# Block 0's x in four slots, its LayerNorm by two, its turns between the rows of shift and scale, and gate's row ahead of a root

## The chip, the core and the metric

The kernel runs on one core of one Trainium2 chip. The metric is the device time of one execution in microseconds. Of the kernel before, three executions took 575.44, 575.63 and 576.18 us; the median is 575.63.

## What is computed

One block of a conditioned network on x of 2 x 2048 x 512 in float32, with a condition of 2 x 512. Six vectors per batch entry come from the condition: shift, scale and gate for each of two halves.

```python
emb = jnp.dot(silu(t), ada_w) + ada_b
shift_msa, scale_msa, gate_msa, shift_mlp, scale_mlp, gate_mlp = jnp.split(emb, 6, axis=-1)
norm = _ln(x) * (1.0 + scale_msa[:, None]) + shift_msa[:, None]
h = gelu(jnp.dot(norm, ssm_w1) + ssm_b1, approximate=False)
x = x + gate_msa[:, None] * (jnp.dot(h, ssm_w2) + ssm_b2)
norm2 = _ln(x) * (1.0 + scale_mlp[:, None]) + shift_mlp[:, None]
hf = gelu(jnp.dot(norm2, ff_w1) + ff_b1, approximate=True)
x = x + gate_mlp[:, None] * (jnp.dot(hf, ff_w2) + ff_b2)
```

`_ln` takes the mean away and multiplies by the reciprocal root of the variance plus 1e-6. `ada_w` is 512 x 3072, the ssm weights are 512 x 512, the ff weights 512 x 1024 and 1024 x 512.

## The kernel before

The 4096 tokens are eight blocks of 512. A block stands as 128 partitions with C = 4 slots of one token each (128 x 4 x 512, 1 MB). Per block there are four products: hA (first ssm weight) and oA (second), then hC and oC for the ff half. Each is computed with seven products of quarters instead of eight (P1 to P7), with sums and differences of quarters formed by DVE and GpSimd ahead of them (nS, hSA, w_s, forms). The hardware order of every engine is the order in which the program is written; the table PLAN says at which product ("P1" and so on) which side work of the first blocks is issued.

What matters here is the beginning, block 0 up to the first product of block 1.

- **Loads.** SP issues them in the order of the program. load_x(0, 2) loads block 0's x in two halves of two slots (line 305). load_ada_01 (348) and load_last_ada_01 (355) load the rows of ada_w for shift and scale of the ssm half, cut by k, a quarter of the 512 rows: k 0 and 1 together, k 2, and k 3 in two halves of columns. Between them come the halves of w1 (323), then x of block 1 (305), gate's columns ada_2 (311), four small rows of gate's bias (376), w2 (318) and so on. ACT issues four small loads of rows into fw2_t: the condition, ada_b, ssm_b1, ff_b1 (336 to 339).
- **Completion counters.** Every transfer counts up one of eight counters (DMAHW0 to DMAHW7), taken in turn over both queues; the issue that takes a counter again stands until the transfer that had it before has landed, and with it everything behind it on SP's queue.
- **Condition.** TensorE turns the 44 rows (1660), ACT copies them to colsT and takes SiLU (1666, 1669). idle matmuls (warm, 1651) keep TensorE busy while it waits. rows_01 (418) multiplies the condition by ada's rows of one k into the bank pada_01; modulation_01 (431, 435) turns the result on DVE and adds the bias, half by half (part 0 wants k 3's first half, part 1 its second).
- **LayerNorm of block 0.** DVE takes statistics per slot (748, 749), n1[0].root() forms variance plus eps (812) and GpSimd raises it to -0.5 (813); first_steps refines the root with four small DVE operations on all four slots (836 to 840). normal writes the normalized slot, on ACT for slots 0 and 2 (876), on DVE for 1 and 3 (880), into blocks. TensorE turns each slot with four matmuls against the identity into the banks pt (911), and modulate scales and shifts from there into nT (932 on ACT, 934 on DVE). h 0 holds slots 0 and 1, h 1 slots 2 and 3.
- **Gate and block 1.** gate_2.0 multiplies the condition by ada_2 on TensorE (397) and adds the bias on DVE (455, result w2_t); gate_2.1 spreads it over the partitions with TensorE (462, pgate), and DVE folds it into w2 (550). n1_1.stats, root, rest, normal, turn, move and modulated are the LayerNorm of block 1: sums and squares on ACT (777, 788), one slot on DVE (748), the root (812, 813), refining steps (853 to 861), normalization (876), turning by DVE in blocks of 32 x 32 (887) and sixteen DMAs (895) instead of TensorE, and modulation (932, 934).

Of the kernel before, what the change touches and what calls it, by code (L numbers as in the profile page):

```python
# [36 lines left out]
F32 = mybir.dt.float32  # L37
AF = mybir.ActivationFunctionType
ALU = mybir.AluOpType
EPS = 1e-06  # L40
# [100 lines left out]
        "P1": "n1_1.stats.0 n1_1.stats.2 n1_0.sum.1 n1_1.stats.1 n1_0.sum.3 n1_1.stats.3",  # L141
        "P2": "n1_0.sum.2 n1_1.stats.4",
        "P5": "n1_1.stats.7 n1_1.stats.6",
        "P6": "n1_1.stats.5 n1_1.root.0 gate_2.0 n1_1.rest.0 n1_1.normal.0",
        "P7": "gate_2.1 n1_1.normal.3 gb_2.0 seed_0.0 gb_2.1 w2.0",
        "P3": "w2.1 seed_0.1 n1_1.turn.0 w2.2 w2.3 w2.4",
        "P4": "n1_1.normal.1 w2.5 n1_1.normal.2",
# [95 lines left out]
def kernel(  # L243
# [57 lines left out]
    def load_x(i, pieces=1):  # L301
        xs[i] = big_tile(f"x_{i}")
        for s in range(pieces):
            c = slice(s * C // pieces, (s + 1) * C // pieces)
            nc.sync.dma_start(out=xs[i][:, c, :], in_=x_blk[i][:, c, :])
# [29 lines left out]
    rows = brows[:ROWS, 2, :P]  # L335
# [76 lines left out]
    def rows_01(pa, ks, hs=range(2)):  # L412

        for k in ks:
            w = ada_01[k // 2][:, k % 2].rearrange("p (g h n m q) -> p h m g n q", g=2, h=2, n=KD // 2, q=G)
            for h in hs:
                for m in range(P // G):
                    nc.tensor.matmul(
                        pa[m * G : (m + 1) * G, h * P : (h + 1) * P],
                        silu[:, k, :],  # L420
                        w[:, h, m],
                        start=(k == 0 and h == 0),
                        stop=(k == KD - 1),
                        tile_position=(0, m * G),
                        skip_group_check=True,
                    )
# [308 lines left out]
    class Norm:  # L735
# [91 lines left out]
            v.tensor_tensor(self.nmr, self.mv[:, :, 0], self.rstd, ALU.mult)  # L827
            v.tensor_scalar(self.nmr, self.nmr, -1.0, None, ALU.mult)

        def first_steps(self):  # L830

            n, v = self.name, nc.vector
            self.rstd, self.nmr = [small.tile([P, C], F32, tag=t, name=f"{t}{n}") for t in ("rstd", "nmr")]
            room = ps_t.tile([P, D], F32, tag="t", name=f"small{n}")
            a, b = room[:, :C], room[:, C : 2 * C]
            v.tensor_scalar(a, self.mv[:, :, 1], EPS, None, ALU.add)
            v.tensor_tensor(b, self.r, a, ALU.mult)
            v.scalar_tensor_tensor(b, b, -0.5, self.r, ALU.mult, ALU.mult)
            v.scalar_tensor_tensor(self.rstd, b, 1.5, self.r, ALU.add, ALU.mult)
            v.scalar_tensor_tensor(self.nmr, self.mv[:, :, 0], -1.0, self.rstd, ALU.mult, ALU.mult)  # L840
# [793 lines left out]
    n1 = {0: Norm(0, 1), 1: Norm(1, 1)}  # L1634
# [14 lines left out]
    def warm(count, blocks=2):  # L1649
        for _ in range(count):  # L1650
            nc.tensor.matmul(
                idle[:, :blocks],
                ident,
                ident.unsqueeze(1).to_broadcast([P, blocks, P]),
                start=True,
                stop=True,
            )

    warm(IDLE - 1, C)
    nc.tensor.transpose(pt[:, :ROWS], rows, ident[:ROWS, :ROWS])  # L1660
# [549 lines left out]
```

## Time and profile before

The profile shows one execution; its own time is 576.39 us, and its span, from the first to the last instruction, is 574.3 us. Names in it lack buffer numbers: x is any block's x, nT any turned block, fw_t is fw2_t, w_t is w2_t.

| | us |
|---|---|
| executions | 575.44, 575.63, 576.18 |
| the profiled execution | 576.39 |
| its span | 574.3 |
| DVE busy | 443.5 |
| ACT busy | 306.2 |
| GpSimd busy | 452.8 |
| DMA: moved, mean rate | 61.79 MB, 108 GB/s |

In the timeline a row has start and length in us, the engine, the line, the operation, output and inputs, and in brackets how long the engine stood idle before it and what it waited for. SPq and ACTq are the queues' issues of DMAs, PEld TensorE's loads of weights. The first 32 us move 11.52 MB, 360 GB/s in the mean; after that the DMA engines are mostly idle.

### The profile page before, as it was taken

How to read it: one execution, taken by the hardware profiler on the slowest of the kernel's cores; microseconds unless marked ns; L12 is line 12 of the kernel's file. 1: busy time of each engine (PE TensorE's matmuls, PEld its weight loads, DVE VectorE, ACT ScalarE, POOL GpSimd, SP SyncE). 2: the span in 40 equal slices, each digit the busy share in tenths (PEclk: the TensorE clock that was granted, in tenths of full speed). 3: DMA queues.
4: the chain of work that ended last, by engine and by line, in shares of the span. 5: the costliest groups of instructions: out<-in, count | busy, mean ns of one | idle time of the engine just before them, and what ended most of it. 6: DMA issues, size and time to landing. Idle time of an engine off the chain costs nothing.

```text
span 574.3 us, 10316 instructions
## 1 busy us (share of the span) xinstructions
PE 568.2 (99%) x3495; PEld 512.4 (89%) x3495; DVE 443.5 (77%) x992; ACT 306.2 (53%) x612; POOL 452.8 (79%) x477
## 2 busy tenths in 40 slices
PE   8999999999999999999999999999999999999997
PEld 4888888898899889998899988998889999899897
DVE  4898899657789376986869877996768588897676
ACT  2628559566834875448724688335655431732430
POOL 1699897996897869897899989998993888379261
PEclk9999999999999999999999999999999999999999
DMA  8968330414305503383032921242240240031002
GB/s 318 392 199 285 93 87 6 98 54 179 68 9 155 212 2 74 102 260 117 1 92 63 349 86 24 51 126 114 92 110 1 111 136 14 0 74 75 0 1 74
DMA packets 26992, 61.79 MB, mean 108 GB/s; under 512 B 5136, under 2 KB 6716, under 8 KB 25276
## 3 DMA queue, kind: packets, MB, share of 16 engines
q1 hardware_dynamic: 23040, 55.67, 30.0%
q10 hardware_dynamic: 3900, 5.47, 3.8%
q8 instruction: 28, 0.46, 0.3%
q14 instruction: 24, 0.20, 0.1%
HBM read 35.42 MB, written 9.97 MB: 79 GB/s over the span
## 4 chain that ended last, share of the span: by engine, by line
PE 97%; DMA 2%; DVE 0%; SPq 0%; ACT 0%; issue 0%; DVEq 0%
PE px_hC L1530 12%; PE pv_hC L1530 10%; PE py_hC L1530 10%; PE py_hA L709 9%; PE pl_oC_A_y L1364 5%; PE pv_hA L709 5%; PE py_oA L1091 5%; PE pl_oC_P_y L1204 4%; PE pl_oC_B_y L1364 4%; PE py_oA L709 4%; PE py_oC L1156 4%; PE pl_oC_A_v L1364 2%; PE px_hA L709 2%; PE pl_oC_P_v L1204 2%; PE pl_oA_y L1106 2%; PE pl_oC_B_v L1364 2%
## 5 line engine op out<-in xcount | busy, mean ns | idle before, releaser
L1435 POOL TENSOR_TENSOR forms<-forms 128x256 f32<-128x256 f32 x64 | 47.0, 735 | 3.8
L813 POOL TENSOR_TENSOR r<-ve,minus_half 128x4 f32<-128x4 f32 x16 | 16.6, 1037 | 41.4 <-DVE ve L812 33.8
L1530 PE MATMUL py_hC<-forms,fw 128*128 128x256 f32 x192 | 46.7, 380 | 0.0
L932 ACT ACTIVATE nT<-nT,mod,mod 128x512 f32<-128x512 f32 x31 | 22.9, 804 | 42.3 <-DMA nT<-blocks 34.3
L1530 PEld LDWEIGHTS py_hC<-forms,fw 128*128 128x128 f32 x192 | 36.3, 190 | 5.2 <-DVE hClo L1547 0.2
L1547 DVE TENSOR_TENSOR hClo<-hClo,py_hC 128x512 f32<-128x512 f32 x46 | 31.1, 682 | 10.6 <-ACT hClo L1544 7.4
L500 POOL TENSOR_TENSOR hSC<-hClo,hChi 128x512 f32<-128x512 f32 x14 | 18.0, 1286 | 27.0 <-ACT hChi L1525 24.8
L876 ACT ACTIVATE nT<-x,nmr,rstd 128x512 f32<-128x512 f32 x33 | 24.9, 804 | 18.8 <-DVE nmr L861 16.6
L1547 DVE TENSOR_TENSOR hChi<-hChi,pv_hC 128x512 f32<-128x512 f32 x38 | 25.2, 677 | 9.6 <-PE pv_hC L1530 5.3
L748 DVE BATCH_NORM_STATS2 st<-x 128x6 f32<-128x512 f32 x41 | 27.7, 677 | 5.6 <-DMA x<-in_x_dram 5.5
L1530 PE MATMUL px_hC<-forms,fw 128*128 128x256 f32 x128 | 31.5, 379 | 0.0
L1525 ACT ACTIVATE hClo<-hClo,colsT 128x256 f32<-128x256 f32 x64 | 28.8, 498 | 5.0 <-DVE hClo L1547 4.8
L1525 ACT ACTIVATE hChi<-hChi,colsT 128x256 f32<-128x256 f32 x64 | 28.7, 496 | 2.9 <-DVE hChi L1547 2.9
L1530 PEld LDWEIGHTS px_hC<-forms,fw 128*128 128x128 f32 x128 | 24.3, 190 | 3.3
L500 POOL TENSOR_TENSOR hClo<-hClo 128x512 f32<-128x512 f32 (+1 forms) x21 | 26.1, 1241 | 0.1
L1547 DVE TENSOR_TENSOR hChi<-hChi,px_hC 128x512 f32<-128x512 f32 x32 | 21.8, 682 | 4.4 <-ACT hClo L1544 2.1
L932 ACT ACTIVATE x<-x,mod 128x512 f32<-128x512 f32 x24 | 17.6, 802 | 13.4 <-DMA x<-blocks 13.4
L887 DVE STREAM_TRANSPOSE blocks<-nT 128x512 f32<-128x512 f32 x36 | 24.0, 691 | 0.7 <-ACT nT L876 0.7
L1530 PE MATMUL px_hC<-forms,fw_s 128*128 128x256 f32 x96 | 23.6, 382 | 0.0
L1544 ACT ACTIVATE hClo<-px_hC 128x512 f32<-128x512 f32 x22 | 13.1, 596 | 19.5 <-PE px_hC L1530 16.0
L1547 DVE TENSOR_TENSOR hClo<-hClo,px_hC 128x512 f32<-128x512 f32 x26 | 17.6, 677 | 7.6 <-PE px_hC L1530 7.0
L1530 PE MATMUL pv_hC<-nT,fw 128*128 128x256 f32 x96 | 23.3, 379 | 0.0
(588 smaller groups left out, 1904.5 us busy)
## 6 DMA issues: line engine op xcount, KB each, us to landing
x<-in_x_dram SPq DMA_DIRECT2D x13, 1024.0 KB
out_dram<-x SPq DMA_DIRECT2D x14, 512.0 KB
x<-blocks SPq DMA_DIRECT2D x93, 64.0 KB
nT<-blocks SPq DMA_DIRECT2D x88, 64.0 KB
ada<-in_L_cond_ada_w_dram SPq DMA_DIRECT2D x5, 1024.0 KB
fw<-in_L_cond_ff_w_dram SPq DMA_DIRECT2D x2, 2048.0 KB
nT<-blocks ACTq DMA_DIRECT2D x56, 64.0 KB
w<-in_L_cond_ssm_w_dram SPq DMA_DIRECT2D x2, 1024.0 KB
```

The lines of the kernel that those rows point to most:

```text
L500: eng.tensor_tensor(out[:, r], a[:, r], b[:, r], f)
L709: nc.tensor.matmul(ps[b][j * apart][:, j, :], lhs(p, j, k), rhs(p, j, k), start=(fresh and j * (not apart) == 0 and k == 0), stop=(p in (" ...
L748: nc.vector.bn_stats(st, xs[self.i][:, c, :])
L876: nc.scalar.activation(t, x_c, AF.Identity, bias=self.nmr[:, c : c + 1], scale=self.rstd[:, c : c + 1])
L932: nc.scalar.activation(dst, src, AF.Identity, bias=shift, scale=scale)
L1091: nc.tensor.matmul(ps[BANK[p]][:, j, :], hops(p, j, k), wops[p][:, k, :], start=False, stop=(k == KD // 2 - 1), skip_group_check=True,)
L1204: nc.tensor.matmul(t[:, n, :], hops.leaves[p][f][:, k, :], leaf_wops[p][f][:, k, :], start=room not in started, stop=(f in ("P2", "P3", "P ...
L1364: nc.tensor.matmul(rooms[g, b][:, at[p], :], hops.leaves[p][f][:, k, :], leaf_wops[p][f][:, k, :], start=(g, b) not in started, stop=(f in ...
L1435: eng.tensor_tensor(reg[d], reg[a], reg[b], ALU.add if f == "+" else ALU.subtract)
L1525: nc.scalar.activation(h, h, AF.Gelu_apprx_tanh, bias=fb1T[:, m : m + 1])
L1530: nc.tensor.matmul(ps[b][:, j, :], fa[ra][:, j * P : (j + 1) * P], fb[rb].rearrange("p a (c q) -> p c a q", q=Q), start=(fresh and j == 0) ...
L1547: nc.vector.tensor_tensor(dest(d), dest(d), ps[b], op)
```

## The change

Five edits. Block 0's x is loaded in four transfers of one slot. The rows of k 0, 1 and 2 become one transfer each. The condition's eight rows are turned by themselves, ahead of the 44, with one idle matmul of 512 columns and one of 128 columns fewer in all, and SiLU reads them from the bank. The root and its refining steps run once for slots 0 and 1 and once for slots 2 and 3, the additions of 1 to colsT go from DVE to GpSimd between the two roots, and on TensorE the turns of slots 1 and 0 go ahead of the rows of k 2, with only slots 3 and 2 behind the first half of k 3. In PLAN, gate_2.0 goes ahead of block 1's root.

```diff
-        "P6": "n1_1.stats.5 n1_1.root.0 gate_2.0 n1_1.rest.0 n1_1.normal.0",
+        "P6": "n1_1.stats.5 gate_2.0 n1_1.root.0 n1_1.rest.0 n1_1.normal.0",
...
-    load_x(0, 2)
+    load_x(0, C)
...
-    load_ada_01((0, 1))
-    load_ada_01((2,))
+    for k in range(KD - 1):
+        load_ada_01((k,))
...
+        def first_root(self, h):
+
+            n, v, s = self.name, nc.vector, slice(h * C // 2, (h + 1) * C // 2)
...
+            v.tensor_scalar(self.ve[:, s], self.mv[:, s, 1], EPS, None, ALU.add)
+            nc.gpsimd.tensor_tensor(self.r[:, s], self.ve[:, s], minus_half[:, s], ALU.pow)
+            v.tensor_scalar(self.first_room[:, s], self.mv[:, s, 1], EPS, None, ALU.add)
...
-    warm(IDLE - 1, C)
+    warm(IDLE - 3, C)
+    turned_cond = pt[:, ROWS : ROWS + B * KD]
+    nc.tensor.transpose(turned_cond, rows[R_COND:R_ADA], ident[: B * KD, : B * KD])
+    warm(1, C)
     nc.tensor.transpose(pt[:, :ROWS], rows, ident[:ROWS, :ROWS])
     warm(1, C)
-    warm(1, 1)
-
-    run(n1[0].stats())
-    n1[0].root()
-    nc.scalar.copy(colsT, pt[:, :ROWS])
...
+    nc.scalar.copy(colsT[:, R_ADA:], pt[:, R_ADA:ROWS])
+
+    stats = n1[0].stats()
+    run(stats[:2])
+    n1[0].first_root(0)
+    run(stats[2:])
+    for g in (1, 4):
+        rows_g = colsT[:, R_ADA + g * KD : R_ADA + (g + 1) * KD]
+        nc.gpsimd.tensor_scalar(rows_g, rows_g, 1.0, None, ALU.add)
+    n1[0].first_root(1)
     w1_ops, w1_sums, w1_s = weight_of_first("w1", w1_sb)
     run(w1_sums)
+    for h in range(2):
+        n1[0].first_steps(h)
+        for c in (3 * h, 1 + h):
+            n1[0].normal(c, nc.vector if c % 2 else None, on_pe=True)
     pada_01 = ps_t.tile([P, D], F32, tag="t", name="pada_01")
-    rows_01(pada_01, (0, 1))
-    for c in range(C):
-        n1[0].normal(c, nc.vector if c % 2 else None, on_pe=True)
...
+    rows_01(pada_01, (0, 1))
+    n1[0].transpose(1, pts, True)
+    n1[0].transpose(0, pts, False)
     rows_01(pada_01, (2,))
-    n1[0].transpose(1, pts, True)
     rows_01(pada_01, (3,), (0,))
-    for c in (0, 3, 2):
-        n1[0].transpose(c, pts, c == 3)
+    n1[0].transpose(3, pts, True)
+    n1[0].transpose(2, pts, False)
```

SP's queue at the start of the program, before; in brackets the completion counter that an issue waits for. The counters not named on SP's first rows went to ACT's four loads.

```order
L305 DMA x_90<-in_x_dram 128x1024 x2
L348 DMA ada_93<-in_L_cond_ada_w_dram 128x2x1024
L348 DMA ada_94<-in_L_cond_ada_w_dram 128x1024
L355 DMA ada_94<-in_L_cond_ada_w_dram 128x2x256 [waits DMAHW0_49]
L323 DMA w_98<-in_L_cond_ssm_w_dram 128x2x512 [waits DMAHW1_49]
L355 DMA ada_94<-in_L_cond_ada_w_dram 128x2x256 [waits DMAHW2_49]
L323 DMA w_98<-in_L_cond_ssm_w_dram 128x2x512 [waits DMAHW3_49]
L305 DMA x_102<-in_x_dram 128x2048 [waits DMAHW4_49]
```

The same place of the changed kernel. Counter 0 is the condition's load, 2 ada_b's, 4 and 5 the two other rows of ACT, 1, 3, 6 and 7 the slots of x.

```order
L305 DMA x_90<-in_x_dram 128x512 x4
L348 DMA ada_95<-in_L_cond_ada_w_dram 128x1024 [waits DMAHW0_49]
L348 DMA ada_95<-in_L_cond_ada_w_dram 128x1024 [waits DMAHW1_49]
L348 DMA ada_96<-in_L_cond_ada_w_dram 128x1024 [waits DMAHW2_49]
L355 DMA ada_96<-in_L_cond_ada_w_dram 128x2x256 [waits DMAHW3_49]
L323 DMA w_101<-in_L_cond_ssm_w_dram 128x2x512 [waits DMAHW4_49]
L355 DMA ada_96<-in_L_cond_ada_w_dram 128x2x256 [waits DMAHW5_49]
L323 DMA w_101<-in_L_cond_ssm_w_dram 128x2x512 [waits DMAHW6_49]
L305 DMA x_105<-in_x_dram 128x2048 [waits DMAHW7_49]
```

The waits begin three transfers earlier: the rows of k 0, 1 and 2, which waited for nothing, now wait for the condition, for x's first slot and for ada_b.

TensorE around the rows of shift and scale, before: pada is the bank of the rows (k 0 and 1, then k 2, then half of k 3), pt the banks of the turned slots, pt_0_0 for slots 0 and 1, pt_0_1 for slots 2 and 3.

```order
L418 MATMUL pada_175<-ada_93,w_t 32x128 x16
L418 MATMUL pada_175<-ada_94,w_t 32x128 x8
L911 MATMUL pt_0_0_0_200<-w_t,blocks_0_193 128x128
L911 MATMUL pt_0_0_1_201<-w_t,blocks_0_193 128x128
...
L418 MATMUL pada_175<-ada_94,w_t 32x128 x4
L911 MATMUL pt_0_0_0_200<-w_t,blocks_0_193 128x128
...
L911 MATMUL pt_0_1_0_202<-w_t,blocks_0_193 128x128
...
L709 MATMUL py_hA_0_245<-nT_0_192,w_98 128x256
```

And of the changed kernel, where ada_95 holds k 0 and 1, ada_96 k 2 and 3:

```order
L418 MATMUL pada_192<-ada_95,w_t 32x128 x16
L921 MATMUL pt_0_0_0_193<-w_t,blocks_0_183 128x128
L921 MATMUL pt_0_0_1_194<-w_t,blocks_0_183 128x128
...
L418 MATMUL pada_192<-ada_96,w_t 32x128 x12
L921 MATMUL pt_0_1_0_195<-w_t,blocks_0_183 128x128
...
L709 MATMUL py_hA_0_254<-nT_0_182,w_101 128x256
```

Eight of the sixteen turning matmuls now stand ahead of the rows of k 2, where none stood, and eight instead of twelve behind k 3's first half.

DVE where block 1's root and gate's row are, in the changed kernel: L1007 reads product P6 of hA, L455 is gate's row, L812 and L863 begin the root's steps.

```order
L1007 TENSOR_TENSOR forms<-py_hA_0_254,colsT 128x2x256 [waits PE_49]
L455 TENSOR_TENSOR w_t<-pada_304,fw_t 128x128 [waits DMAHW3_49,DMAHW2_49,DMAHW4_49,DMAHW1_49,PE_49]
L812 TENSOR_SCALAR ve_1_322<-mv_1_270 128x4 [waits DVE_49,Activation_49]
L863 TENSOR_SCALAR small_1_328<-mv_1_270 128x4
L867 TENSOR_TENSOR small_1_328<-r_1_323,small_1_328 128x4 [waits DVE_49,Pool_49]
```

Before, L812, which waits for ACT's statistics, stood ahead of L455.

More of the change, by code (lines that the diff above doesn't have):

```diff
@@ L828, in rest, with first_steps @@
             v.tensor_scalar(self.nmr, self.nmr, -1.0, None, ALU.mult)
[L830 to L840, printed above, removed]
+        def first_root(self, h):
+            n, v, s = self.name, nc.vector, slice(h * C // 2, (h + 1) * C // 2)
+            if h == 0:
+                self.ve, self.r, self.rstd, self.nmr = [
+                    small.tile([P, C], F32, tag=t, name=f"{t}{n}") for t in ("ve", "r", "rstd", "nmr")
+                ]
+                self.first_room = ps_t.tile([P, D], F32, tag="t", name=f"small{n}")
+            v.tensor_scalar(self.ve[:, s], self.mv[:, s, 1], EPS, None, ALU.add)
+            nc.gpsimd.tensor_tensor(self.r[:, s], self.ve[:, s], minus_half[:, s], ALU.pow)
+            v.tensor_scalar(self.first_room[:, s], self.mv[:, s, 1], EPS, None, ALU.add)
+        def first_steps(self, h):
+            v, s = nc.vector, slice(h * C // 2, (h + 1) * C // 2)
+            a, b = self.first_room[:, :C][:, s], self.first_room[:, C : 2 * C][:, s]
+            r, rstd, nmr = self.r[:, s], self.rstd[:, s], self.nmr[:, s]
+            v.tensor_tensor(b, r, a, ALU.mult)
+            v.scalar_tensor_tensor(b, b, -0.5, r, ALU.mult, ALU.mult)
+            v.scalar_tensor_tensor(rstd, b, 1.5, r, ALU.add, ALU.mult)
+            v.scalar_tensor_tensor(nmr, self.mv[:, s, 0], -1.0, rstd, ALU.mult, ALU.mult)
         def steps(self, scratch=None):
@@ L1657, in warm @@
             )
-    warm(IDLE - 1, C)
+    warm(IDLE - 3, C)
+    turned_cond = pt[:, ROWS : ROWS + B * KD]
+    nc.tensor.transpose(turned_cond, rows[R_COND:R_ADA], ident[: B * KD, : B * KD])
+    warm(1, C)
     nc.tensor.transpose(pt[:, :ROWS], rows, ident[:ROWS, :ROWS])
     warm(1, C)
-    warm(1, 1)
-    run(n1[0].stats())
-    n1[0].root()
-    nc.scalar.copy(colsT, pt[:, :ROWS])
     nc.scalar.activation(
         silu[:, :, :B].rearrange("p k b -> p b k"),
-        colsT[:, R_COND:R_ADA].rearrange("p (b k) -> p b k", b=B),
+        turned_cond.rearrange("p (b k) -> p b k", b=B),
         AF.Silu,
     )
-    n1[0].first_steps()
+    nc.scalar.copy(colsT[:, R_ADA:], pt[:, R_ADA:ROWS])
[7 more added lines that the diff above has]
+    n1[0].first_root(1)
     w1_ops, w1_sums, w1_s = weight_of_first("w1", w1_sb)
     run(w1_sums)
+    for h in range(2):
+        n1[0].first_steps(h)
+        for c in (3 * h, 1 + h):
+            n1[0].normal(c, nc.vector if c % 2 else None, on_pe=True)
     pada_01 = ps_t.tile([P, D], F32, tag="t", name="pada_01")
-    rows_01(pada_01, (0, 1))
-    for c in range(C):
-        n1[0].normal(c, nc.vector if c % 2 else None, on_pe=True)
-    for g in (1, 4):
-        rows_g = colsT[:, R_ADA + g * KD : R_ADA + (g + 1) * KD]
-        nc.vector.tensor_scalar(rows_g, rows_g, 1.0, None, ALU.add)
     pts = {
```

## The prediction

> **What bounds the kernel now.** First the busy times and TensorE's waits, from the page and the view of waits (engine line waited for: us in total, times, longest):
>
> ```profile
> PE 568.2 (99%) x3495; PEld 512.4 (89%) x3495; DVE 443.5 (77%) x992; ACT 306.2 (53%) x612; POOL 452.8 (79%) x477
> PE rowsT L1660 <- DMA fw_t<-in_L_cond_ff_b_dram: 1.1, 1, 1.1
> ```
>
> TensorE works 568.2 of 574.3 us, and the change touches only the first 45 us. So the question is by how much the start of that dense stretch moves, and whether something else then stops it. The chain of work for the first 45 us (start, us, what):
>
> ```profile
> 2.10 9.07 DMA ada<-in_L_cond_ada_w_dram
> ...
> 11.22 0.64 PE pada L418 x16
> 11.86 0.59 PE pt L911 x4
> 12.45 0.36 PE pada L418 x8
> 12.80 1.47 PE pt L911 x12
> ...
> 14.95 0.69 DVE nS L500
> ...
> 16.12 0.57 ACT nT L932
> ...
> 16.74 1.99 PE px_hA L709 x8
> ```
>
> I call this chain A: the ada rows land, TensorE multiplies them (pada), turns x slots (pt), DVE and ACT modulate, and from px_hA at 16.74 TensorE no longer waits visibly. But a view that follows one releaser hides a second chain of nearly the same length, B. I looked for it in the timelines, engine by engine, at the next place where TensorE needs new data, block 1's first product at 43.65:
>
> ```profile
> 17.95 0.63 ACT L777 ACTIVATE unread<-x 128x512 f32<-128x512 f32 x1 [0.81 <-DMA x<-in_x_dram]
> ...
> 24.23 0.17 DVE L812 TENSOR_SCALAR ve<-mv 128x4 f32<-128x4 f32 x1 [1.32 <-ACT unread L788]
> 24.44 0.29 DVE L455 TENSOR_TENSOR w_t<-pada,fw_t 128x128 f32<-128x128 f32 x1
> 24.48 1.02 POOL L813 TENSOR_TENSOR r<-ve,minus_half 128x4 f32<-128x4 f32 x1 [1.20 <-DVE ve L812]
> 24.95 1.05 PE L462 MATMUL pgate<-w_t,fw_t 128*128 128x128 f32 x8
> 25.54 0.17 DVE L857 TENSOR_TENSOR small<-r,small 128x4 f32<-128x4 f32 x1 [0.74 <-POOL r L813]
> ...
> 28.69 0.68 DVE L550 TENSOR_TENSOR w<-w,pgate 128x512 f32<-128x512 f32 x1
> 29.30 1.89 PE L709 MATMUL py_oA<-w,forms 128*128 128x256 f32 x8
> 33.96 1.29 DVE L887 STREAM_TRANSPOSE blocks<-nT 128x512 f32<-128x512 f32 x2
> 35.28 5.44 SPq L895 DMA_DIRECT2D nT<-blocks  x8
> ...
> 42.78 2.23 ACT L932 ACTIVATE nT<-nT,mod 128x512 f32<-128x512 f32 x3 [10.59 <-DMA fw_t<-in_L_cond_ada_b_dram]
> 43.65 1.38 PEld L709 LDWEIGHTS py_hA<-nT,w 128*128 128x128 f32 x7 [0.42 <-ACT nT L932]
> ```
>
> B begins when block 1's x lands (17.9), and every member starts when the one before ends: ACT's statistics, DVE's ve, GpSimd's root r, DVE's normalization and turns, the 16 moves, the modulation, and the weight load at 43.65, which stood 0.42 us idle for ACT. Is there slack inside B? The view by stretches says no (busy us of PE, PEld, DVE, ACT, POOL; clock, DMA share, GB/s):
>
> ```profile
> 1.60:4.80 3.20, 3.20 (x4) 1.26 (x5) 0.00 (x0) 1.49 (x2) 0.13 (x1) 1.00 0.87 251
> 4.80:7.20 2.40, 2.40 (x5) 0.77 (x3) 1.64 (x4) 0.00 (x0) 0.00 (x0) 1.00 1.01 390
> 5.00:8.00 3.00, 2.28 (x5) 0.69 (x3) 2.24 (x6) 0.00 (x0) 0.00 (x0) 1.00 1.02 398
> 17.95:24.20 6.25, 6.25 (x57) 5.18 (x56) 4.47 (x7) 6.19 (x15) 5.33 (x5) 1.00 1.05 386
> 18.00:20.50 2.50, 2.50 (x13) 2.20 (x12) 2.26 (x4) 2.45 (x8) 2.50 (x3) 1.00 1.05 388
> 25.54:35.25 9.71, 9.71 (x49) 8.60 (x48) 9.61 (x20) 5.73 (x10) 5.95 (x5) 1.00 0.78 302
> ```
>
> ACT is busy 6.19 of 6.25 us from x's landing to the last statistic, DVE 9.61 of 9.71 from the root to the last turn. And the DMA engines are full (share about 1.0) from 4.8 on, so x of block 1 lands when the bytes ahead of it in the queue are through. **A and B meet at 43.65; the later one sets the end.**
>
> **The change part by part.** My sum is against the profiled execution: span 574.3, its own time 576.39, so 2.1 us lie around the span. That run was 0.76 slower than the median of 575.63; I carry the difference over to the median.
>
> *Turns ahead of the rows of shift and scale (chain A).* Before, 12 turns (1.47 us) stand behind the last rows. Now those of slots 1 and 0 (c1, c0) stand between the rows of k 0, 1 and those of k 2, and only c3's and c2's, 8 of 12, stand behind. From chain A: k 1's rows end about 10.5 (0.54, half of the 1.08 in the row at 9.96 below, after a landing near 9.9); 8 turns 0.98 to 11.5, by when k 2's rows have landed (11.2); k 2's multiplications 0.6 to 12.1, k 3's 0.36 to 12.45 instead of 12.81; the last 8 turns to 13.45 instead of 14.27.
>
> ```profile
> 9.96 1.08 PE L418 MATMUL pada<-ada,w_t 128*32 128x128 f32 x32
> 11.14 1.52 ACT L876 ACTIVATE blocks<-x,nmr,rstd 128x512 f32<-128x512 f32 x2 [2.02 <-DVE nmr L840]
> 13.49 1.27 ACT L932 ACTIVATE nT<-pt,mod 128x256 f32<-128x256 f32 x2 [0.82 <-PE pt L911]
> ```
>
> The modulation's first read of pada moves from 12.8, right behind that product, to about 12.5, ACT's first modulation from 13.49 to 13.1, the difference sum nS from 14.95 to 14.45 (behind ACT's two, 1.27 us). **So A gains 0.35 us at the first product (14.10) and 0.5 at px_hA.** It would lose part of that if k 3's first half landed later than 12.1; the matmul at 12.45 shows only that it had landed by then.
>
> *x in four slots, statistics by two.* The normalized slots must be ready by 10.5 (c1, c0) and 12.45 (c3, c2).
>
> ```profile
> 7.23 0.69 DVE L748 BATCH_NORM_STATS2 st<-x 128x6 f32<-128x512 f32 x1 [0.66 <-DMA x<-in_x_dram]
> 11.15 1.00 DVE L880 TENSOR_SCALAR blocks<-x,rstd,nmr 128x512 f32<-128x512 f32 x2
> L828 POOL TENSOR_SCALAR nmr<-nmr 128x4 f32<-128x4 f32 x1 | 0.2, 236 | 0.1
> ```
>
> x's last bytes landed at 7.2 and still do, but only the fourth slot's statistics (0.69 and 0.2 behind it) are left then: two small operations more, and at 8.4 DVE starts the first pair's four steps (0.2 each), whose root is done by then, since slots 0 and 1 land before the last two. c1 is written by 9.75 (0.5 each in the row at 11.15), c0 by ACT (0.76 each, row at 11.14) by 10.0. The second pair's root stands on GpSimd behind two additions on colsT, which wait for the turned rows; those (8.35, quoted with rival 2) let them start near 9.0, at 0.24 each as in L828, so the root starts at 9.5. On 2 columns instead of 4 it costs between nothing and the 1.02 of L813; I take 1.02, the same operation. Steps from 10.5, c3 and c2 by 12.1. Cover is left in both places, 0.5 and 0.35 us; beyond it, A would lose what is missing. DVE loses the additions, GpSimd has nothing else until 15.4.
>
> *More, smaller transfers (chain B).* Four pieces of 256 KB and rows of 2048 bytes replace two of 512 KB and rows of 4096; ada's first piece becomes two. That is three issues more on SP (0.43 each), hidden: the engines have a backlog. What does count is the engines' time, for every byte behind moves with it. The stretch 5 to 8 has rows of 4096 bytes at 398 GB/s, 18 to 20.5 rows of 2048 at 388: for 1.05 MB that is 2.70 instead of 2.63, +0.07. Three more completions I put at 0.03 together. The ends: −1.1 (the slow first stretch, 251 instead of 390 GB/s over 3.2 us, disappears) and +1.1 (it is paid twice). I take the near row: **x of block 1 lands 0.1 later, and B with it.**
>
> A page speaks against this part: the Trainium skill, "DMA: Bandwidth & Descriptors", section "Rules for kernel authors", wants 128 partitions and at least 1 MiB per DMA for full bandwidth, and its section on the anatomy of a DMA (GpSimd's path) has a fixed 2.0 us for each. Here, halves of 512 KB follow one another at 398 GB/s in the trace, so the fixed part lies under the next transfer; by the page taken as serial, x would need four times 2.6 us, estimated.
>
> *Gate's row ahead of the root.* DVE's L455 (0.29) goes from behind L812 to ahead of it. L812 waited for ACT until 24.23 anyway, so there is nothing for B. For A it matters: L455 would end near 23.5, and TensorE's gate product (24.95), earlier by A's gain, would otherwise wait for 24.73. Cost zero; if TensorE's rows of the gate came later than 24.2, it would delay the root.
>
> *Sum.* Behind the gate, TensorE reaches py_oA (29.30) up to 0.5 earlier, but its second slice needs DVE's fold that ends at 29.37, a member of B, so already there at most about 0.3 is left. At 43.65 B decides: TensorE is early and waits for a modulation 0.1 later than before. **576.39 + 0.1 = 576.5; in terms of the median, 575.7.**
>
> **The rivals.**
>
> *1, A's gain lasts.* If x of block 1 lands earlier by as much as A gains, the 0.3 to 0.5 us arrive at the end: 575.2. It needs a faster start of the queue; the first stretch has room for up to 1.1. Against it: same bytes, same order.
>
> *2, SP starves the queue (slower).* SP's issues, in order:
>
> ```profile
> 0.72 0.86 SPq L305 DMA_DIRECT2D x<-in_x_dram  x2
> ...
> 6.88 0.37 SPq L355 DMA_DIRECT2D ada<-in_L_cond_ada_w_dram  x1
> ...
> 8.35 0.23 PE L1660 MATMUL rowsT<-w_t,fw_t 44*128 44x44 f32 x1 [1.08 <-DMA fw_t<-in_L_cond_ff_b_dram]
> ```
>
> The issue at 6.88 stood until ada_b's rows had landed (its completion counter's last user). In the changed order that same landing holds k 2's issue, with everything behind it. Ahead of it are x and k 0, 1, 2.1 MB: 0.80 by 4.8, 0.94 more by 7.2, the rest at 393 GB/s by 8.1. From an issue to its first bytes takes about 1 us (0.72 against the 1.6 slice). So the point is 7.1: with 6.85, as before, nothing; if the rows land as late as the ff rows did, 8.2, the engines stand idle 1.1 us, A and B lose it, and the result is 576.9.
>
> *3, a cold clock (slower).* TensorE's warm-up is one matmul shorter ahead of the rows:
>
> ```profile
> 5.77 0.24 PEld L1651 LDWEIGHTS idle<-w_t 128*128 128x128 f32 x1 [0.52 <-issue]
> 6.26 0.19 PEld L1651 LDWEIGHTS idle<-w_t 128*128 128x128 f32 x1 [0.24 <-issue]
> 8.51 1.35 PE L1651 MATMUL idle<-w_t 128*128 128x512 f32 x4
> ```
>
> Up to 5.77 a load stood 0.52 us idle behind the slow matmul ahead of it, from 6.26 on 0.24: the array speeds up there, and behind the 1.08 us gap its four pieces (8.51) take 0.34 each, still fast. Now three matmuls end near 6.3, and the gap to 8.35 could be 2.1 us. If it falls back, 3.7 us of work up to 12.45 take some 1.3 more, A exceeds B by about 0.9, and the end is 576.6. The Trainium skill, "TensorE: Matmul & The Clock Gate", section "Part 1: The HAM clock gate", drops the clock after an idle window of about 3.4 us; by that this gap is safe, and the trace shows only that 1.08 is.
>
> *4, small transfers at the page's serial price.* Block 0's x would end 3 us or more later (four fixed parts, where the trace hides them): 578.7.
>
> That the change does not do what it says is excluded by the listed order.
>
> **How the numbers follow.** The forecast, 575.7 with B as the bound, gets 0.62 (its own range 575.2 to 576.2: ±0.3 is the spread of the three runs, the rest the unknown start of the queue). Rival 1 gets 0.20, 2 gets 0.07, 3 gets 0.04, 4 gets 0.01, a start of the queue over 1 us faster 0.06. A measurement of this kernel can tell about 0.2%, 1.15 us, from no change, so "faster" is below 574.5 and "slower" above 576.8; rivals 1 and 3 stay within. Faster 0.06, same 0.86, slower 0.08. The range 574.9 to 576.8 leaves out a part of rival 2, rival 4 and the very fast start.
>
> **What would show it.** Right: px_hA starts near 16.2, ACT's first unread (17.95) at 18.0 or a little later, DVE's ve at 24.3, and the weight load at 43.65 idle longer than 0.42 for ACT. Wrong: ACT's unread at 17.5 or earlier and the load's wait gone (rival 1); a gap in GB/s between 7 and 10 with SP's third ada issue after 7.1 (2); pada loads at half pace after the rows' turn (3). If px_hA does not move at all, my reading of A is wrong: then k 3's landing, not the turns, held the chain.

## The result, and the profile after

The changed kernel takes **578.12 us** (median of six runs, 577.33 to 579.18) against 575.95 before (six runs, 575.44 to 576.18): ratio 1.0041, 95% interval 1.0029 to 1.0052. It is slower by 2.2 us, where I had forecast no change and a range up to 576.8. Its profiled execution took 578.14, span 576.4, so 1.7 us lie around the span.

First the busy times and TensorE's waits after (the page; then engine line waited for: us in total, times, longest):

```profile
PE 567.8 (99%) x3492; PEld 511.3 (89%) x3492; DVE 443.6 (77%) x996; ACT 305.8 (53%) x612; POOL 453.8 (79%) x480
PE pada L418 <- DMA ada<-in_L_cond_ada_w_dram: 2.9, 2, 2.3
PE py_hA L709 <- DMA w_s<-park_w: 0.4, 1, 0.4
PE py_hA L709 <- ACT nT L942: 0.3, 1, 0.3
```

The work is the same; the wait is new. Before, TensorE waited 0.2 us in all for the ada rows, now 2.9. The view by stretches says why (busy us of PE, PEld, DVE, ACT, POOL; clock, DMA share, GB/s), of the changed kernel:

```profile
1.60:4.80 3.20, 3.20 (x4) 0.91 (x4) 0.83 (x2) 1.49 (x2) 0.13 (x1) 1.00 0.71 219
4.80:7.20 2.40, 2.40 (x6) 1.12 (x6) 1.85 (x6) 0.13 (x2) 0.71 (x1) 1.00 0.92 258
7.20:9.80 2.60, 0.82 (x2) 0.00 (x0) 1.03 (x3) 0.13 (x2) 0.42 (x2) 1.00 1.02 409
1.60:7.20 5.60, 5.60 (x9) 2.03 (x10) 2.68 (x7) 1.62 (x4) 0.84 (x2) 1.00 0.80 236
```

From 4.8 to 7.2 the queue moved 258 GB/s where it had moved 390, and from 7.2 on it ran at full rate again. Over 1.6 to 7.2 that is 236 against 310 GB/s before:

```profile
1.60:7.20 5.60, 5.60 (x8) 2.03 (x8) 1.64 (x4) 1.49 (x2) 0.13 (x1) 1.00 0.93 310
```

5.6 us times 74 GB/s are 0.41 MB, or 1.06 us at the 390 GB/s of a full queue, and the loads that start both chains, the rest of ada's rows for A and block 1's x for B, stand behind those bytes. Members of A and B in the timelines after:

```profile
8.91 0.69 DVE L748 BATCH_NORM_STATS2 st<-x 128x6 f32<-128x512 f32 x1 [1.53 <-DMA x<-in_x_dram]
10.34 0.65 PE L418 MATMUL pada<-ada,w_t 128*32 128x128 f32 x16 [2.31 <-DMA ada<-in_L_cond_ada_w_dram]
17.79 1.92 PE L709 MATMUL px_hA<-nT,w 128*128 128x256 f32 x8
19.64 0.63 ACT L777 ACTIVATE unread<-x 128x512 f32<-128x512 f32 x1 [1.52 <-DMA x<-in_x_dram]
24.24 0.29 DVE L455 TENSOR_TENSOR w_t<-pada,fw_t 128x128 f32<-128x128 f32 x1 [0.30 <-PE pada L397]
25.92 0.17 DVE L812 TENSOR_SCALAR ve<-mv 128x4 f32<-128x4 f32 x1 [1.39 <-ACT unread L788]
45.09 1.89 PE L709 MATMUL py_hA<-nT,w 128*128 128x256 f32 x8
```

The last slot of block 0's x lands at 8.9 (7.2 before), the ada rows late enough to leave TensorE 2.31 us idle, px_hA moves from 16.74 to 17.79, block 1's x from 17.95 to 19.64, and block 1's first product from 43.65 to 45.09: 1.44 of the span's 2.1 us. Another 0.37 is the wait for w_s at 325; that wait is not owed to the pieces, since h2 below has 0.4 of it with x in halves and i2 has none with x in quarters. The rest is spread behind.

That first product is the mark that all runs share. Span minus its start is 530.2 to 531.5 us in all 18 profiles of this study, so whatever a run changes ahead of 45 us shows in the time, give or take 0.7.

### The profile page after: what moved, and what is told of

It reads as the page before. It is cut to its first block, busy times and chain, and to the rows that moved or that the text cites. A ratio compares the mean times of both kernels' runs of the same rounds, so it can differ in the third digit from the quotient of the medians.

```text
span 576.4 us, 10323 instructions
## 1 busy us (share of the span) xinstructions
PE 567.8 (99%) x3492; PEld 511.3 (89%) x3492; DVE 443.6 (77%) x996; ACT 305.8 (53%) x612; POOL 453.8 (79%) x480
## 4 chain that ended last, share of the span: by engine, by line
PE 93%; DMA 3%; ACT 1%; ACTq 1%; DVE 1%; issue 0%; DVEq 0%
PE px_hC L1540 12%; PE pv_hC L1540 10%; PE py_hC L1540 10%; PE py_hA L709 10%; PE py_oA L1101 4%; PE pv_hA L709 4%; PE pl_oC_A_y L1374 4%; PE pl_oC_P_y L1214 4%; PE py_oA L709 4%; PE py_oC L1166 4%; PE pl_oC_B_y L1374 3%; PE px_hA L709 2%; PE pl_oC_P_v L1214 2%; PE pl_oA_y L1116 2%; PE pl_oC_A_v L1374 2%; PE py_oC L1314 2%
## 5 line engine op out<-in xcount | busy, mean ns | idle before, releaser
L1535 ACT ACTIVATE hClo<-hClo,colsT 128x256 f32<-128x256 f32 x64 | 28.8, 498 | 5.0 <-DVE hClo L1557 4.8
L1554 ACT ACTIVATE hClo<-px_hC 128x512 f32<-128x512 f32 x22 | 13.1, 596 | 19.5 <-PE px_hC L1540 16.0
```

The costliest lines, as they stand in the source:

```text
L1535: nc.scalar.activation(h, h, AF.Gelu_apprx_tanh, bias=fb1T[:, m : m + 1])
```

## The experiments

The table holds what the traces show: the time (median, with how many runs), the kernel before on the same chip, GB/s from 4.8 to 7.2, the start of px_hA (A), the start of block 1's first product, and the difference of these two.

| run | us (runs) | before | GB/s | px_hA | product | diff. |
|---|---|---|---|---|---|---|
| before | 575.95 (6) | | 390 | 16.74 | 43.65 | 26.91 |
| changed | 578.12 (6) | 575.95 | 258 | 17.79 | 45.09 | 27.30 |
| e1, x in halves | 575.63 (11) | 575.72 | 384 | 15.75 | 43.44 | 27.69 |
| e2, only x in quarters | 577.86 (5) | 575.72 | 258 | 17.27 | 44.25 | 26.98 |
| e3, ada joined | 579.68 (5) | 575.72 | 268 | 19.87 | 46.82 | 26.95 |
| e4, both loads as before | 575.89 (11) | 575.72 | 381 | 15.90 | 43.22 | 27.32 |
| g1, x by partitions | 581.24 (1) | 575.59 | 204 | 21.71 | 48.44 | 26.73 |
| g2, x in slot pairs | 576.21 (1) | 575.59 | 372 | 17.18 | 43.91 | 26.73 |
| g3, x whole | 577.18 (1) | 575.59 | 402 | 16.87 | 43.60 | 26.73 |
| g4, before again | 575.69 (1) | 575.59 | 397 | 16.01 | 42.76 | 26.75 |
| h1, block 1's x in quarters | 575.70 (10) | 575.82 | 351 | 16.31 | 43.05 | 26.74 |
| h2, e1 + block 1's x in halves | 575.59 (12) | 575.82 | 400 | 15.76 | 42.42 | 26.66 |
| h3, x in three | 576.65 (1) | 575.82 | 304 | 17.08 | 43.81 | 26.73 |
| h4, x on two queues | 582.78 (1) | 575.82 | 358 | 23.15 | 49.89 | 26.74 |
| i1, ada ahead of x quarters | 578.47 (1) | 575.83 | 273 | 18.36 | 45.20 | 26.84 |
| i2, changed + warm-up | 577.02 (11) | 575.83 | 259 | 17.46 | 44.80 | 27.34 |
| j1, quarters, rows on SP | 577.63 (1) | 575.83 | 292 | 18.07 | 44.80 | 26.73 |
| j2, halves, rows on SP | 576.51 (1) | 575.83 | 366 | 16.80 | 43.76 | 26.96 |

### Which load? (e1 to e4)

Theory X: four pieces of x slow the queue. Rival S: SP's issues of ada's single k's, each behind a wait, leave it thin.

```diff
 # e1, against the changed kernel
-    load_x(0, C)
+    load_x(0, 2)
 # e2, against the kernel before
-    load_x(0, 2)
+    load_x(0, C)
 # e3, against the changed kernel (e4 is e1 and e3 together)
-    for k in range(KD - 1):
-        load_ada_01((k,))
+    load_ada_01((0, 1))
+    load_ada_01((2,))
```

> The changed kernel, but block 0's x comes in two pieces of 512 KB again (rows of 4096 bytes); ada still in single k's, turns, statistics and gate as changed. Theory X (four pieces of x with rows of 2048 bytes slow the queue in its first 7 us, and both chains start later): the stretch 4.8 to 7.2 is back near 390 GB/s instead of 258, ACT's first unread on block 1 near 18.0 instead of 19.64, px_hA near 16.3 instead of 17.79, time 575.2 to 576.2. Theory S (SP's issues of ada's k 1 and k 2, each waiting for an earlier landing, leave the queue thin): the stretch stays near 260 GB/s, unread near 19.5, time 577.5 to 578.5.

> The kernel before, with one edit: block 0's x in four pieces of 256 KB. Theory X: 4.8 to 7.2 falls from 390 to about 260 GB/s, unread from 17.95 to about 19.5, time 577.0 to 578.3. Theory S: with ada's first piece still one issue of 1 MB the queue is not thin, 4.8 to 7.2 stays above 350 GB/s, unread at 18.0 to 18.3, time 575.7 to 576.3.

> The changed kernel, but ada's k 0 and k 1 in one issue of 1 MB again; x still in four pieces. Theory X: nothing returns, 4.8 to 7.2 near 260 GB/s, unread near 19.5, time 577.5 to 578.5. Theory S: the stretch recovers, unread near 18.2, time 575.4 to 576.4.

> The changed kernel with both loads as before (x in two pieces, ada's k 0 and k 1 in one); only the turns' order, statistics by two and gate's row are left of the change. Both theories: the queue is as before (390 GB/s in 4.8 to 7.2, unread near 18.0). If chain B binds as I predicted, px_hA near 16.3 and yet the time as before, 575.5 to 576.1; if A's gain lasts, 575.2 to 575.5; if the in-order statistics of the last slots hold the first normalized slots back, px_hA at 16.7 or later.

X holds, S falls. Taking the four pieces away brings the whole loss back (e1: ratio to before 1.0002, 0.9993 to 1.0010); adding them alone makes it (e2: 1.0046, 1.0033 to 1.0060). The stretch of e1, then of e2:

```profile
1.60:7.20 5.60, 5.48 (x8) 1.70 (x8) 2.34 (x7) 1.49 (x2) 0.51 (x2) 1.00 0.94 318
```

```profile
1.60:7.20 5.60, 5.60 (x8) 2.20 (x8) 2.50 (x6) 1.49 (x2) 0.13 (x1) 1.00 0.85 233
```

One expectation of e2 missed: block 1's x, where 19.5 was expected, lands at

```profile
18.49 0.63 ACT L777 ACTIVATE unread<-x 128x512 f32<-128x512 f32 x1 [0.81 <-DMA x<-in_x_dram]
```

That is 1.15 us before the changed kernel, with the same loss in the queue. By its landing 5.8 MB have moved in e2 and 6.3 MB in the changed kernel, so more bytes of other transfers came in ahead of it there. The pieces of x account for the queue's loss, then, but only for a part of the late landing; what adds the rest is not shown.

e3 missed both expectations: 579.68, slower than the changed kernel. With k 0 and k 1 joined, no row of ada is there before both are, and TensorE's gap grows from 2.31 to 3.87 us. Its timeline, and its stretches with the clock:

```profile
11.45 1.59 PE L418 MATMUL pada<-ada,w_t 128*32 128x128 f32 x32 [3.87 <-DMA ada<-in_L_cond_ada_w_dram]
12.97 1.97 PE L921 MATMUL pt<-w_t,blocks 128*128 128x128 f32 x8
```

```profile
7.60:11.40 3.80, 0.00 (x0) 0.00 (x0) 2.38 (x10) 0.62 (x1) 0.73 (x1) 1.00 1.02 400
11.40:15.20 3.80, 3.75 (x48) 3.05 (x52) 1.03 (x4) 1.01 (x2) 0.00 (x0) 0.56 1.08 398
```

The granted clock falls to half for some 3.4 us behind the gap, and eight turns take 1.97 instead of 1.09 us. All five runs of e3 have a mean granted clock of 0.994 to 0.997; so do two of the changed kernel's six (578.72 and 579.18, at 0.997; its others, at 1.000, are 577.33 to 578.14) and two of e2's five (579.23 and 579.58). None of the runs of the kernel before in these comparisons is below 0.999. Only one of these runs with a fallen clock was profiled, that of e3.

### The clock's share (i2)

```diff
     nc.tensor.transpose(pt[:, :ROWS], rows, ident[:ROWS, :ROWS])
-    warm(1, C)
+    warm(3, C)
```

> The changed kernel with two more warm-up matmuls (1.12 us each) behind the turn of the rows, so that TensorE's gap ahead of the first pada row, 2.31 us in the profile, closes to about 0.1. If the upper half of the changed kernel's runs (578.7 and 579.2, mean granted clock 0.997) comes from the clock falling in that gap, no run here shows 0.997, the highest stays under 578.6 and the median falls to 577.3 to 577.9. If the clock plays no part, the median stays at 578.1 with runs up to 579.

No run of i2 shows less than 0.999, the highest is 577.85, and the median 577.02 lies below the expectation; ratio 1.0019 (1.0010 to 1.0028). The gap did not close to 0.1, since the two matmuls add 1.7 us (six pieces in 2.84 us instead of two in 1.12), not 2.2, but it shrank from 2.31 to 0.85:

```profile
10.03 0.64 PE L418 MATMUL pada<-ada,w_t 128*32 128x128 f32 x16 [0.85 <-DMA ada<-in_L_cond_ada_w_dram]
```

So with no fall of the clock in any run the kernel is still 1.2 us slower than before, and about 1 of the 2.2 us goes with the gap. The fall explains the two high runs of the changed kernel. Its four others, at 577.33 to 578.14 and a clock of 1.000, also lie above i2's median, and i2's lowest, 576.48, lies 0.85 below their lowest; the fall does not explain that, and it stays open.

### Pieces, rows or place? (g1 to g3, h1, h3, h4, i1)

```diff
 # all against the kernel before; g1, g2, g3, h3 and h4 replace this line
-    load_x(0, 2)
 # g1
+    for s in range(4):
+        nc.sync.dma_start(out=xs[0][s * 32 : (s + 1) * 32], in_=x_blk[0][s * 32 : (s + 1) * 32])
 # g2
+    for s in range(2):
+        nc.sync.dma_start(out=xs[0][:, s::2, :], in_=x_blk[0][:, s::2, :])
 # g3
+    load_x(0)
 # h3
+    for c in (slice(0, 2), slice(2, 3), slice(3, 4)):
+        nc.sync.dma_start(out=xs[0][:, c, :], in_=x_blk[0][:, c, :])
 # h4
+    for c in range(C):
+        eng = nc.scalar if c % 2 else nc.sync
+        eng.dma_start(out=xs[0][:, c : c + 1, :], in_=x_blk[0][:, c : c + 1, :])
 # h1
-    load_x(1)
+    load_x(1, C)
 # i1
-    load_x(0, 2)
...
     load_ada_01((0, 1))
+    load_x(0, C)
```

> The kernel before, with block 0's x again in four pieces of 256 KB, but each piece is 32 partitions with all their four slots (8 KB in a row in memory) instead of one slot of 128 partitions. Theory N (the number of pieces, or their size, slows the queue): 4.8 to 7.2 near 260 GB/s and the last of x after 8.2, as in the runs with four slots. Theory R (what slows it is the shape: 128 rows of 2 KB, 8 KB apart): 4.8 to 7.2 at 375 GB/s or more, the last of x near 7.2. The time means little here, since the statistics wait for all four pieces.

> The kernel before, with x in two pieces of 512 KB as before, but the first holds slots 0 and 2, the second 1 and 3, so that rows are 2 KB, 4 KB apart, instead of 4 KB. Theory N: two pieces as before, so 375 GB/s or more in 4.8 to 7.2, time near 575.7. Theory R: slow, 4.8 to 7.2 between 260 and 340 GB/s and x's last bytes later than 7.8.

> The kernel before, with x in one piece of 1 MB. If each piece costs the start of the queue something, the first stretch, 1.6 to 4.8, is above the 251 to 268 GB/s seen with two pieces, and 4.8 to 7.2 is 385 or more. If the pieces play no part, the first stretch stays near 260 GB/s. The time gets worse by the later statistics (they start at about 6.5 instead of 5), so only the rates count.

> The kernel before, with block 1's x (not block 0's) in four pieces of 256 KB. It is issued when the queue is full. Theory N as a price of every piece (about 0.4 us each, from the 1.2 us that the last three pieces of block 0's x took each where 0.67 us are the bytes): its last bytes land 1.2 us or more later than in the runs with one piece (17.2 to 17.9), chain B loses, time 576.5 or more. Theory N as a price at the start of the queue only: the last bytes land within 0.2 us of before, ACT's first unread starts up to 1.9 us earlier (three quarters of 2.7 us) since it needs one slot only, and the time is 575.2 to 575.8.

> The kernel before, with x in three pieces: slots 0 and 1 together, then 2 and 3 alone. Loss in proportion to the pieces: 4.8 to 7.2 between 300 and 360 GB/s (half of the way from 390 to 260). If only the first pieces of the queue are dear, as 390: 380 or more, since the first piece is as large as before.

> The kernel before, with x in four pieces of 256 KB, slots 0 and 2 issued by SP, 1 and 3 by ACT behind its four issues of rows. If one queue hands its pieces over one after another at about 1.2 us each and two queues do it side by side, 4.8 to 7.2 is at 370 GB/s or more. If four pieces of 2 KB rows cost the engines themselves, it stays near 260.

> The kernel before, with ada's first piece (1 MB, rows of k 0 and 1) ahead of block 0's x in the queue, and x in four pieces of 256 KB behind it. If the price of the four pieces lies in the start of the queue (they follow one another before the next one is ready), they now have 2.6 us of another transfer's bytes to get ready under: 4.8 to 7.2 at 375 GB/s or more. If block 0's slots themselves are slow to read or to write, 4.8 to 7.2 stays below 320. The time means little, since x lands 2.6 us later.

The number of pieces counts: with one, two, three and four the stretch from 4.8 to 7.2 has 402, 351 to 400 (six profiles), 304 and 258 to 268 GB/s (e2, e3, i2 and the changed kernel). Rows of 2 KB in two pieces (g2) leave it at 372, just under the 375 expected for the number alone. But they start late, with 198 GB/s in 1.6 to 4.8, and over the whole stretch they lose as well:

```profile
1.60:7.20 5.60, 5.60 (x8) 2.12 (x8) 1.17 (x3) 1.49 (x2) 0.13 (x1) 1.00 0.82 273
```

Here halves with rows of 4 KB have 299 to 322 (six profiles), quarters 233 to 248. So the rows of 2 KB, which come with the quarters, are a rival for a good part of the loss, and these runs do not separate them from the number of pieces: a run of four pieces with rows of 4 KB is missing. g1 does not help to tell: its pieces go to 32 partitions each and move at 204, and the 16 moves of block 1, also 32 partitions each, run at about 200 as well. h4 missed (358, not 370): the two pieces on ACT's queue landed at 10.2 and 12.3, behind the first of SP's ada rows, and TensorE waited 3.9 us for the normalized slots.

h1 settles that a small piece with rows of 2 KB is not dear as such. Four quarters of the same shape, issued into a full queue, in the view by stretches and in ACT's timeline:

```profile
15.00:18.00 3.00, 2.91 (x14) 2.25 (x13) 2.93 (x7) 2.30 (x7) 2.88 (x3) 1.00 1.05 388
16.61 0.63 ACT L777 ACTIVATE unread<-x 128x512 f32<-128x512 f32 x1
```

388 GB/s, with the first slot ready 0.6 to 1.3 us earlier than a whole x. But the start of the queue is not the answer either. In i1 the quarters come behind 1 MB of ada:

```profile
5.00:6.50 1.50, 1.50 (x5) 0.64 (x3) 0.00 (x0) 0.00 (x0) 0.00 (x0) 1.00 0.73 226
6.50:8.00 1.50, 0.88 (x4) 0.36 (x3) 0.69 (x1) 0.12 (x1) 0.00 (x0) 1.00 1.00 374
```

One hole at 5.0 to 6.5, and the later slots near full rate. The 273 GB/s of 4.8 to 7.2 is below 320, as the theory of slow slots had it, and yet the same slots pass at 374 behind it: so neither theory of that run holds. In this run the price falls on the first 1.5 us of the pieces and not on each of them.

### ACT's queue beside it (j1, j2)

What is under way beside the pieces at the start, and not later, are the four loads of rows on ACT's queue. In i1 TensorE still waits for them at 7.6.

```diff
 # against the kernel before; the first of four such loads, the others alike; x in j1: load_x(0, C)
-    nc.scalar.dma_start(out=rows[R_COND:R_ADA, :], in_=cond.rearrange("b (k p) -> (b k) p", p=P))
...
     load_x(0, 2)
+    nc.sync.dma_start(out=rows[R_COND:R_ADA, :], in_=cond.rearrange("b (k p) -> (b k) p", p=P))
```

> The kernel before with x in four pieces, and the four small loads of rows (512 bytes each row) issued by SP behind x, where ACT's queue carried them beside x. If the price of the pieces comes from the second queue (each piece's end has to wait for the small transfers beside it), 4.8 to 7.2 is at 350 GB/s or more and x's fourth slot lands before 7.3. If the second queue plays no part, 4.8 to 7.2 stays at 300 or less. The time means little: the rows land later.

> The same with x in two pieces as before, for comparison. If the second queue costs the start of every kernel of this family something, the first stretch, 1.6 to 4.8, is above 300 GB/s instead of 251 to 268. If not, it stays there; 4.8 to 7.2 is about 390 less what the four small loads cost in their place.

DVE's statistics start as the slots land. In e2, and then in j1:

```profile
3.92 0.69 DVE L748 BATCH_NORM_STATS2 st<-x 128x6 f32<-128x512 f32 x1 [3.92 <-DMA x<-in_x_dram]
5.29 0.69 DVE L748 BATCH_NORM_STATS2 st<-x 128x6 f32<-128x512 f32 x1 [0.45 <-DMA x<-in_x_dram]
6.41 0.69 DVE L748 BATCH_NORM_STATS2 st<-x 128x6 f32<-128x512 f32 x1 [0.22 <-DMA x<-in_x_dram]
7.81 0.69 DVE L748 BATCH_NORM_STATS2 st<-x 128x6 f32<-128x512 f32 x1 [0.49 <-DMA x<-in_x_dram]
```

```profile
3.85 0.69 DVE L748 BATCH_NORM_STATS2 st<-x 128x6 f32<-128x512 f32 x1 [3.85 <-DMA x<-in_x_dram]
4.73 0.69 DVE L748 BATCH_NORM_STATS2 st<-x 128x6 f32<-128x512 f32 x1
5.56 0.66 DVE L748 BATCH_NORM_STATS2 st<-x 128x6 f32<-128x512 f32 x1
6.85 0.70 DVE L748 BATCH_NORM_STATS2 st<-x 128x6 f32<-128x512 f32 x1 [0.42 <-DMA x<-in_x_dram]
```

With ACT's queue empty, slots 1 and 2 are there before DVE is free, and the last slot is there at 6.85 instead of 7.81 (8.6 to 8.9 in the three other profiles with quarters at the head of the queue), before the 7.3 expected. But the rate does not come back: 292 GB/s from 4.8 to 7.2 lies on the other side, the 300 or less of a second queue that plays no part. The four small loads now stand in SP's queue, yet in j2, with halves and the same loads there, the stretch has 366, and over 1.6 to 7.2 it has 312 against j1's

```profile
1.60:7.20 5.60, 5.60 (x8) 2.27 (x8) 2.82 (x7) 0.61 (x2) 0.13 (x1) 1.00 0.90 264
```

So quarters still lose 48 of the 74 GB/s with ACT's queue empty. In the changed kernel, too, TensorE turns the 44 rows at 6.71, so that ACT's loads had landed 2.2 us before the last slot did. In j2 the first stretch stays at 271: the second queue costs halves next to nothing. ACT's loads beside the pieces are at most a part of the price, on one profile each. What makes x in four pieces slow at the start of the queue is not shown, only that it is, and that the same pieces behind a full queue are not (h1).

### Which chain binds? (g4, h2)

```diff
 # h2, against e1 (g4 is the kernel before, unchanged)
-    load_x(1)
+    load_x(1, 2)
```

> The kernel before, unchanged, for a second profile: how far the stretches and landings move from one execution to the next. Expected: first stretch 245 to 270 GB/s, 4.8 to 7.2 at 380 to 395, ACT's first unread on block 1 between 17.2 and 18.0, px_hA 16.5 to 16.9. If unread comes at 17.3 here too, the 0.7 us by which it was early in the runs with two pieces is scatter; if it comes at 17.9, the shorter wait of SP's queue made it.

> The changed kernel with block 0's x in two pieces, and block 1's x in two pieces as well: A as in the first run of this series (px_hA near 15.8), and B begins one piece (up to 1.3 us) earlier. If B is what holds the first product of block 1 once A is early, that product, 43.4 there with 0.97 us of waiting, comes near 42.7 and the time near 574.9 to 575.2, below both kernels. If B starts earlier and the product does not move, something else holds it (the 16 moves, which took 7.0 to 8.0 us in the profiles so far), and the time stays at 575.5 to 575.9.

The table's last column answers it. Where TensorE runs without waiting from px_hA on, the product follows 26.66 to 26.75 us later, in nine of the profiles. What is more goes with chain B in the traces that were followed. In e1 it is 27.69, with this row of its weight loads:

```profile
43.44 1.59 PEld L709 LDWEIGHTS py_hA<-nT,w 128*128 128x128 f32 x8 [0.97 <-ACT nT L942]
```

A was 1.0 us early there against the profile before, and B left 0.2 of it. In the changed kernel (27.30) the weight load of that product does not wait at all. There B holds TensorE back earlier, by 0.57 us in all, most of it at two places:

```profile
27.98 0.68 DVE L1024 TENSOR_TENSOR forms<-py_hA,forms 128x512 f32<-128x512 f32 x1
28.77 1.59 PEld L709 LDWEIGHTS py_hA<-nS,w 128*128 128x128 f32 x8 [0.46 <-issue]
30.71 1.59 PEld L709 LDWEIGHTS py_oA<-w,forms 128*128 128x128 f32 x8 [0.34 <-ACT py_oA L673]
```

DVE's L1024 and ACT's L673 have nothing to do with block 1's x, but in program order they stand behind the steps of its root, which end at 28.06. That the first of the two loads waits for L1024 to have read py_hA is read from the times (28.66, then 28.77), since the view names no releaser. i2 (27.34) has the same two waits. In h2, with B moved ahead (ve at 23.03), the wait of e1 is gone:

```profile
23.03 0.17 DVE L812 TENSOR_SCALAR ve<-mv 128x4 f32<-128x4 f32 x1 [0.53 <-ACT unread L788]
```

and the product starts at 42.42, the earliest of all and near the 42.7 expected. In the time it shows less than the 574.9 to 575.2 that went with it: 575.59 (574.92 to 579.22, one run with the clock at 0.994), ratio 1.0000 (0.9989 to 1.0012). h2 beats the changed kernel, not the one before. The run with the fallen clock has x in halves, so the fall also comes without four pieces; that run was not profiled.

g4 shows what one profile is worth here. The unchanged kernel had ACT's unread at 17.24 instead of 17.95, px_hA at 16.01 instead of 16.74, the product at 42.76 without a wait.

## Why the prediction was wrong, point by point

**"More, smaller transfers" is the step that failed.** I put four pieces at 0.1 us, by rows from 18 to 20.5 us where the queue was full. The bytes were right and the neighbour was wrong: the row that resembled the place was the unexplained first stretch, 251 GB/s, which I had quoted and used as a bound only. Measured: 1.06 us of queue, and a landing of block 1's x 1.69 us later (0.54 in e2, where only the pieces were changed; the landing of the unchanged kernel differs by 0.71 between its two profiles). e1 and e2 show that x in four pieces is what costs the time; why it does so at the start of the queue stays open. My upper end, +1.1 ("paid twice"), was the queue's loss almost to the tenth, but I let it into the range as if it reached the time undiminished and alone. The clock came on top in part of the runs, and the sum had no term for it. The profile also has 0.4 us of waiting for w_s at 325, which is not the pieces'.

**"Here, halves follow one another at 398, so the fixed part lies under the next transfer"** was true of halves and did not carry over to quarters at the start of the queue. The sections of the Trainium skill that I weighed ("DMA: Bandwidth & Descriptors", "Rules for kernel authors", which wants 1 MiB per DMA, and the anatomy of a DMA on GpSimd's path with 2.0 us fixed for each) pointed the right way: g3's single 1 MB gave the fastest start, 311 and then 402 GB/s. As a serial price it is too much, since the slots of e2 follow one another 1.1 to 1.4 us apart where the bytes take 0.67, and in h1 it is not there at all. The 578.7 of that rival, to which I gave 0.01, lies nearest to the result, but by luck: it put the end of x 3 us or more later without a sum, x's last slot landed 1.7 later, and about 1 us of the measured loss goes with TensorE's gap (i2).

**Rival 3, the cold clock,** happened in part of the runs, and as far as the runs show by another cause. I looked for it in the shorter warm-up; e2 has the longer warm-up of before and the fall in two of five runs, and in e3 and i2 the fall comes and goes with the gap that the late ada rows leave. The Trainium skill, "TensorE: Matmul & The Clock Gate", "Part 1: The HAM clock gate", has the clock fall after an idle window of about 3.4 us; a gap of 2.31 was safe in the changed kernel's profile and one of 3.87 was not in e3, which agrees. g1, in the last section, does not: there the clock fell with no gap longer than 2.06.

**Rival 2, SP starving the queue,** did not happen: ada_b's rows held k 2's issue for 0.7 us only, and SP had issued k 2 by 5.3, before the point at 7.1. (Its price: 575.7 and 1.1 are 576.8, not the 576.9 that I wrote.)

**Turns ahead of the rows** was mis-sized. With the ada rows starting at the same time (9.25 in e4, 9.27 in g4) px_hA is at 15.90 and 16.01: 0.11 gained, not 0.5, and the first product is 0.14 later, not 0.35 earlier. That product follows the last pada row by 1.3 to 1.4 us in both, as in the profiles before and after, through DVE's transposition of pada and the modulation; the turns behind the rows that I counted stood beside that chain. g4 and e4 are two single profiles, so the 0.11 is within their scatter.

**Statistics by two** were ready later than I put them. The last bytes of x, which were to land at 7.2 as before, landed at 8.9. In e1 DVE writes c1 by 10.06 (9.75 forecast), and TensorE waits 0.5 us for it. In the changed kernel the first pair's steps stand on DVE behind the last slot's statistics, so c3's landing at 8.9 held c1 and c0 as well: they start at 11.0. The root on two columns takes 0.71 us, below the 1.02 that I took.

**Gate's row ahead of the root** costs B nothing, as said: L455 ran at 24.24, ve waited for ACT until 25.92.

**"A and B meet at 43.65; the later one sets the end"** held in e1 and e4, where the gain of A was lost to B as forecast. In the changed kernel the sign that I had named, a longer wait of that weight load for ACT, did not come: the load did not wait, A's 1.05 us of delay at px_hA arrived in full, and B added its part at 28.8 and 30.7, through instructions that stand behind its root. The margin was also only 0.2 us in one profile; in g4, of the same kernel, A was the later one.

## What to carry to other kernels

Splitting a load to start its consumer sooner cost nothing where the queue already had a backlog (h1), and has to be measured where a kernel starts. A price per transfer should be taken from the stretch of the trace where the transfer will stand, even if that stretch is not understood, and a delay at the start should be checked against the length of TensorE's gap, since the clock can fall to half behind it, as in e3. Before a gain on one chain is counted, measure the distance between two marks without waits in several profiles: what exceeds the shortest has to be looked for in the other chain, and not only at the place where the two meet.

## What the runs showed that I had not expected

The clock also fell in g1, where TensorE's longest gap was 2.06 us, and stayed at half for nearly 7 us. Its timeline and stretches:

```profile
10.73 2.29 PE L420 MATMUL pada<-ada,w_t 128*32 128x128 f32 x48 [2.06 <-DMA ada<-in_L_cond_ada_w_dram]
```

```profile
9.80:12.40 2.60, 1.54 (x44) 1.30 (x48) 1.97 (x8) 0.00 (x0) 0.40 (x1) 0.92 1.02 380
12.40:17.90 5.50, 4.06 (x33) 2.89 (x26) 2.85 (x11) 2.08 (x3) 2.22 (x3) 0.50 1.04 397
```

It fell at about 12.0, while the rows were being multiplied, so the length of one gap does not tell alone.

The slots of x that were split by partitions (g1) moved at 204 GB/s, about half of the 381 to 400 of most profiles with halves. The 16 moves of block 1 took 6.95 to 7.99 us from their first issue to ACT's first modulation, a scatter of 1 us inside chain B; the unchanged kernel alone has 7.21 and 7.50.
